# A four-layer kernel on one core: the last batch's matrix made in batch 4, batch 14's outputs in two pairs of tiles

## The chip, the core and the metric

The kernel runs on one core of one Trainium2 chip. The metric is device time in microseconds (us) of one execution, given as the median of several runs. All times below are us unless marked otherwise.

## What is computed

`x` has 16 batches of 512 rows (steps) and 512 columns (features), `cond` 16 rows of 512. Four layers follow each other, each added to its input:

```python
x = x + L0(x, cond)   # a gate from cond; the rest of the layer collapses to x * gate per batch and feature
x = x + L1(x, cond)   # recurrence: h_t = tanh(x_t @ Wx + b + h_{t-1} @ Wh), 512 steps
x = x + L2(x, cond)   # gated recurrence, written with cumulative sums over the steps
x = x + L3(x, cond)   # every batch has its own 512 x 512 matrix
```

L2 and L3, cut to what matters here (LN, GELU and biases inside `h` left out):

```python
f, i = sigmoid(x @ W_f.T + b_f), sigmoid(x @ W_i.T + b_i)
s = f + i + EPS;  f, i = f / s, i / s
new = i * (x @ W_h.T + b_h)
hidden = scans over the steps of f and new            # products and sums along time
layer[b] = base_layer + x_a[b] @ x_b[b].T             # rank 8, x_a and x_b from cond
out[b] = x[b] + x[b] @ layer[b]
```

## The kernel before

Everything is held with features on the 128 partitions, in four chunks of 128 (`KC = 4`), and steps or batches along the free dimension. `x2` (all batches, after L0 and L1) stays in SBUF as `[128, 4, 16, 512]`.

**The recurrence** takes the first 907 us. It also computes L3's factors (`x_a`, `x_b`) and parks them in DRAM, and computes the gates of L2 for the first 128 to 192 steps of each batch ("early"), which are parked in DRAM too. `made_before(b, j)` tells how many steps of batch b and feature chunk j are done so. At its end it makes the matrix of batch 0 in `wx_sb`, whose first use is over. Twice the unit matrix is added to `base_sb`'s diagonal, so that the product with it also carries the residual.

**After the recurrence** a loop over the batches works on L2 and L3. Its order is written by hand in the loop; the tile framework then places the instructions of each engine, whose order the built program fixes. The parts:

- `gate_unit(b, j, x3)`, written (b,j) here: TensorE does three groups of four matrix products into banks `pf`, `pi` and `pc0` or `pc1` (L700; `pc` alternates with j), for the steps that are not early: 384, 384, 368 and 352 columns in units 0 to 3 of batches 1 to 7, and 320 in units 0 and 1 from batch 8 on. SP loads the early steps of f and i (L715), ScalarE makes the sigmoids (L716), VectorE sums, inverts, multiplies and scans (L717 to L732; `f` has three buffers, `i` and `s` two), and GpSimd (POOL) adds (L736) and makes chunk j of `x3`, the input of L3 (L737). In the very last unit VectorE does L736 and L737.
- `layer_rows(b)`: eight small loads by SP of the factors of batch b into `at` and `bt`, which have one buffer each (L527, L528).
- `layer_of(b, at, bt, layer)`: four TensorE products (L535) of 8 rows into the banks `pl0`, `pl1`, `po0`, `po1`, and four VectorE additions of `base_sb` (L539), which write the four chunks of the batch's matrix.
- `last_layer(b, x3, layer)`: four output tiles t of 128 steps. For each, four products over the feature chunks k (L756) into bank `po0` (t even) or `po1` (t odd), a copy by ScalarE to one of two `osb` buffers (L751) and a store by SP (L752). A bank must be copied before it is written again, and an `osb` buffer stored.

PSUM has eight banks, one tile each: `pl0 pf pl1 pi po0 pc0 po1 pc1`. Where a bank is written again, its last reader must be done; where `pl` and `po` banks are used for a matrix, that reader is L539.

The order in batch b from 1 to 14: `layer_rows(b)`, (b,0), (b,1), outputs of batch b - 1, (b,2), `layer_of(b)` into `wx_sb`, (b,3). In batch 15: (15,0), `layer_rows(15)` and `layer_of(15)` into `base_sb` itself, (15,1), (15,2), (15,3), and then the outputs of batch 14. After the loop, batch 15's own outputs: three tiles and two half tiles take their first three feature chunks each (`pl_last`, `po_last`, `po_end`, `pi_end`), then each its last chunk, with copies and stores behind. ScalarE, VectorE, GpSimd and SP each run their instructions in order: a waiting one holds up all behind it.

Of the kernel before, what the change touches and what calls it, by code (L numbers as in the profile page):

```python
# [35 lines left out]
P = 128  # L36
B, S, D = 16, 512, 512
KC = D // P
# [45 lines left out]
def kernel(  # L84
# [41 lines left out]
    base_sb = keep.tile([P, KC, D], F32)  # L126
# [97 lines left out]
    with tc.tile_pool(name="ps_pre", bufs=1, space=PSUM) as ps_pre:  # L224
# [63 lines left out]
        def turned_layer(src, w_sb, which, name, between):  # L288

            ps = ps_pre.tile([P, P], F32, tag="pre", name=f"ps_{name}")  # L290
            for k in range(KC):
                for j in range(KC):
                    nc.tensor.matmul(
                        ps[j * BP : (j + 1) * BP, :],
                        src(k),
                        tile_columns(w_sb[:, k, :], j),
                        start=(k == 0),
                        stop=(k == KC - 1),
                        skip_group_check=True,
                    )  # L300
            between()
            z = pre.tile([P, KC, BP], F32, name=f"z_{name}")
            nc.vector.transpose(z, ps.rearrange("p (c f) -> p c f", c=KC))
            nc.vector.tensor_tensor(z, z, vector_of(which), ALU.add)
            gate = pre.tile([P, KC, BP], F32, name=f"gate_{name}")
            nc.scalar.activation(gate, z, AF.Sigmoid)
            return z, gate
# [26 lines left out]
        _, gate = turned_layer(lambda k: hq[:, k, :], w2_sb, C_L0B2, "g", scale)  # L334
# [189 lines left out]
    def load_layer(b, at, bt):  # L524
        for c in range(KC):
            rows = slice(c * BP, c * BP + R)
            nc.sync.dma_start(out=at[rows, :], in_=factor[0][b, :, c * P : (c + 1) * P])  # L527
            nc.sync.dma_start(out=bt[rows, :], in_=factor[1][b])  # L528
        return at, bt

    def make_layer(at, bt, banks):

        for c, pl in enumerate(banks):
            rows = slice(c * BP, c * BP + R)
            nc.tensor.matmul(pl, at[rows, :], bt[rows, :], start=True, stop=True)  # L535

    def add_base(banks, layer):
        for c, pl in enumerate(banks):
            nc.vector.tensor_tensor(layer[:, c, :], pl, base_sb[:, c, :], ALU.add)  # L539
# [25 lines left out]
    for n in range(NBLK):  # L565
        ahead = []
        if n + 2 < NBLK:
            xs.append(new_x1(n + 2))
        for s in range(T):
# [36 lines left out]
            bank, place = PLACE[g]  # L606
# [7 lines left out]
            if n == 0 and s == G - 1:  # L614
                opening.close()
                x2pool = ctx.enter_context(tc.tile_pool(name="x2pool", bufs=1, side="right"))
                x2 = x2pool.tile([P, KC, B, S], F32)
# [17 lines left out]
            if s in (1, 3) and n < 2 * KC:  # L635
# [3 lines left out]
                if i < 3 * KC:  # L639
                    m, which = divmod(i, 3)  # L640
                    w_sb, w = ((wf_sb, wfT), (wi_sb, wiT), (wc_sb, wcT))[which]
                    j = (KC - 2, KC - 1, 0, 1)[m]
                    at = slice(j * P, (j + 1) * P)
                    nc.scalar.dma_start(out=w_sb[:, :, at], in_=chunks(w)[:, :, at])
                else:
                    k = i - 3 * KC
# [44 lines left out]
    def bank(tag, name):  # L691
        return pools[tag].tile([P, D], F32, tag=tag, name=f"{tag}_{name}")
# [46 lines left out]
    def layer_rows(b):  # L739
        at = work.tile([P, P], F32, tag="at", name=f"at_{b}", bufs=1)  # L740
        bt = work.tile([P, D], F32, tag="bt", name=f"bt_{b}", bufs=1)
        return load_layer(b, at, bt)

    def layer_of(b, at, bt, layer):
        banks = [bank(tag, f"{b}_layer") for tag in ("pl0", "pl1", "po0", "po1")]
        make_layer(at, bt, banks)
        add_base(banks, layer)

    def leave(b, t, po, tag="osb"):
        osb = work.tile([P, D], F32, tag=tag, name=f"osb_{b}_{t}")  # L750
        nc.scalar.copy(osb, po)  # L751
        nc.sync.dma_start(out=out[b, t * P : (t + 1) * P, :], in_=osb)  # L752

    def output_part(po, t, x3, layer, ks):
        for k in ks:
            nc.tensor.matmul(  # L756
                po, x3[:, k, t * P : (t + 1) * P], layer[:, k, :], start=(k == 0), stop=(k == KC - 1)
            )

    def last_layer(b, x3, layer):  # L760
        for t in range(S // P):
            po = bank(f"po{t % 2}", f"{b}_{t}")
            output_part(po, t, x3, layer, range(KC))
            leave(b, t, po)

    layer = wx_sb
    pending = None
    for b in range(B):
        x3 = x3pool.tile([P, KC, S], F32, tag="x3", name=f"x3_{b}")
        end = b == B - 1  # L770
        if 0 < b < B - 1:
            factors = layer_rows(b)
        for j in range(KC):
            gate_unit(b, j, x3)
            if j == (KC - 1 if end else 1) and pending is not None:
                last_layer(*pending)
            if j == 2 and 0 < b < B - 1:
                layer_of(b, *factors, layer)
            if j == 0 and end:

                layer_of(B - 1, *layer_rows(B - 1), base_sb)
        pending = b, x3, layer


# [3 lines left out]
    columns = [slice(n * D // 2, (n + 1) * D // 2) for n in range(2)]  # L788

    def last_rows(ks, n):  # L790
        for k in ks:
            nc.tensor.matmul(
                ends[n],
                x3[:, k, last * P :],
                base_sb[:, k, columns[n]],
                start=(k == 0),
                stop=(k == KC - 1),
            )

    for t, po in enumerate(pos):  # L800
        output_part(po, t, x3, base_sb, range(KC - 1))
    for n in range(2):
        last_rows(range(KC - 1), n)

    for t, po in enumerate(pos):
        output_part(po, t, x3, base_sb, (KC - 1,))
        leave(B - 1, t, po, ("osb", "i", "s")[t])
    for n, copy in enumerate((nc.vector.tensor_copy, nc.scalar.copy)):
        last_rows((KC - 1,), n)
        osb = work.tile([P, D // 2], F32, tag=("s", "osb")[n], name=f"osb_end_{n}")  # L810
        copy(osb, ends[n])
        (nc.sync, nc.scalar)[n].dma_start(out=out[B - 1, last * P :, columns[n]], in_=osb)
# [58 lines left out]
```

## Time and profile before

| what | value |
|---|---|
| three runs, median (lowest to highest) | 1618.64 (1617.01 to 1619.62) |
| the profiled execution | 1615.84 |
| its span (first to last instruction) | 1614.1 |
| the recurrence ends, (0,0) begins on TensorE | 909.4 |
| one batch, by TensorE (batches 1 to 7, then 8 to 14) | 45.0, then 42.4 to 42.9 |
| VectorE busy, 900 to 1600, of 20 in a slice | 12.8 to 19.9 |
| granted TensorE clock | 1.00 throughout |

How to read the profile lines shown below. A group or timeline line gives the start, the duration, the engine, the source line (L539 is line 539), the operation, output <- inputs by the program's names, shapes, and the count. What stands in brackets at the end is how long the engine had been idle before it and whose end released it. PE is TensorE, DVE VectorE, ACT ScalarE, POOL GpSimd, SPq the queue of SP's transfers, whose row is the issue and not the landing. In the list of waits a line reads: engine and line that waited, `<-` engine, tile and line that ended the wait: total us, how many, the longest. Each f32 matrix product shows as two records, so x32 is sixteen products. Records of TensorE overlap a little; from start to start is the better measure.

### The profile page before, as it was taken

The numbers are of one execution on the slowest core, as the hardware profiler recorded it, in microseconds if no ns is written. First come the engines' busy times: TensorE is split into PE (matmuls) and PEld (weight loads), VectorE is DVE, ScalarE is ACT, GpSimd is POOL, SyncE is SP. The second block draws the span as 40 slices with busy tenths as digits, with TensorE's granted clock in tenths as the row PEclk, the third lists the DMA queues.
The fourth block names the chain that finished last, engine by engine and source line by source line (L and its number), as shares of the span: only waits on it lengthen the run. The fifth ranks groups of instructions, "written<-read, shape, count | busy, mean of one in ns | idle before, by whom it ended". The sixth has DMA issues, their size and how long they took to land.

```text
span 1614.1 us, 67901 instructions
## 1 busy us (share of the span) xinstructions
PE 1603.6 (99%) x29328; PEld 1146.0 (71%) x29328; DVE 1132.3 (70%) x3618; ACT 424.9 (26%) x2484; POOL 172.6 (11%) x145
## 2 busy tenths in 40 slices
PE   9999999999999999999999999999999999999998
PEld 6888888888888888888888655555555555555564
DVE  4555655565556666666665798888888888988887
ACT  3333333333333333333333211111111111111111
POOL 0000000000000000000000022222222222222222
PEclk9999999999999999999999999999999999999999
DMA  7554431111111111111111101111111111111111
GB/s 228 148 147 128 121 105 46 36 31 36 37 37 37 37 37 37 37 37 31 37 39 30 29 21 43 33 43 39 43 40 44 44 46 39 31 44 47 37 44 58
DMA packets 128085, 88.11 MB, mean 55 GB/s; under 512 B 22645, under 2 KB 116633, under 8 KB 127785
## 3 DMA queue, kind: packets, MB, share of 16 engines
q1 hardware_dynamic: 79152, 55.05, 11.1%
q10 hardware_dynamic: 48632, 28.73, 6.2%
q8 instruction: 229, 3.75, 1.0%
q14 instruction: 72, 0.58, 0.1%
HBM read 55.67 MB, written 28.07 MB: 52 GB/s over the span
## 4 chain that ended last, share of the span: by engine, by line
PE 96%; DVE 2%; DMA 1%; issue 0%; SPq 0%; ACT 0%; ACTq 0%; DVEq 0%
PE pre L417 41%; PE po L756 13%; PE pg L465 13%; PE pf L700 9%; PE pc L700 9%; PE pi L700 9%; PE pf L380 1%; PE pl_layer L535 1%; DVE s L718 1%; DMA wh_sb<-in_wh_dram 1%; PE pl_last L756 0%; DMA xb<-in_xT_dram 0%; DVE s L726 0%; DVE s L730 0%; PE po_last L756 0%
## 5 line engine op out<-in xcount | busy, mean ns | idle before, releaser
L417 PEld LDWEIGHTS pre<-wh_sb,h_out 128*32 128x32 f32 x16384 | 466.7, 110 | 146.6 <-DVE h_out L610 143.4
L417 PE MATMUL pre<-wh_sb,h_out 128*32 128x128 f32 x16384 | 560.6, 273 | 2.4 <-DVE h_out L610 1.1
L610 DVE STREAM_TRANSPOSE h_out<-a 128x32 f32<-128x32 f32 x2048 | 264.6, 187 | 347.4 <-ACT a L609 345.9
L609 ACT ACTIVATE a<-pre 128x32 f32<-128x32 f32 x2048 | 238.0, 203 | 573.4 <-PE pre L417 572.7
L417 PE MATMUL pre<-wx_sb,x 128*32 128x128 f32 x8192 | 285.9, 273 | 1.0 <-DMA wx_sb<-in_wx_dram 0.5
L417 PEld LDWEIGHTS pre<-wx_sb,x 128*32 128x32 f32 x8192 | 239.0, 110 | 2.1 <-DMA wx_sb<-in_wx_dram 1.5
L756 PE MATMUL po<-wx_sb,x 128*128 128x512 f32 x480 | 209.0, 592 | 0.1
L756 PEld LDWEIGHTS po<-wx_sb,x 128*128 128x128 f32 x480 | 91.0, 190 | 111.6 <-issue 105.7
L700 PE MATMUL pf<-x,wf_sb 128*128 128x352 f32 (+3 forms) x512 | 165.3, 466 | 0.3 <-DVE x L622 0.3
L700 PE MATMUL pc<-x,wc_sb 128*128 128x352 f32 (+3 forms) x512 | 163.7, 463 | 1.3 <-DVE i L722 1.3
L700 PE MATMUL pi<-x,wi_sb 128*128 128x352 f32 (+3 forms) x512 | 163.6, 462 | 0.0
L718 DVE RECIPROCAL s<-s 128x368 f32<-128x368 f32 (+2 forms) x64 | 152.2, 2378 | 2.2
L700 PEld LDWEIGHTS pf<-x,wf_sb 128*128 128x128 f32 x512 | 96.0, 190 | 68.4 <-issue 15.8
L736 POOL TENSOR_TENSOR s<-s,f 128x512 f32<-128x512 f32 x63 | 86.5, 1374 | 509.9 <-DVE s L730 504.1
L700 PEld LDWEIGHTS pc<-x,wc_sb 128*128 128x128 f32 x512 | 97.2, 190 | 57.5 <-DVE i L722 1.9
L700 PEld LDWEIGHTS pi<-x,wi_sb 128*128 128x128 f32 x512 | 97.3, 190 | 55.9
L622 DVE TENSOR_TENSOR x<-x,h_out 128x128 f32<-128x128 f32 x256 | 101.2, 395 | 18.9 <-DMA wi_sb<-in_wiT_dram 0.2
L751 ACT COPY osb<-po 128x512 f32<-128x512 f32 x60 | 35.1, 585 | 263.4 <-PE po L756 144.9
L683 POOL MEMSET zero<- 128x1 f32 x1 | 0.1, 98 | 907.5 <-DVE wx_sb L539 907.5
L717 DVE SCALAR_TENSOR_TENSOR s<-f,i 128x368 f32<-128x368 f32 (+2 forms) x64 | 34.7, 543 | 88.1 <-ACT i L716 88.1
L716 ACT ACTIVATE f<-pf,vec_sb 128x368 f32<-128x368 f32 (+2 forms) x64 | 35.7, 558 | 215.2 <-PE pf L700 160.6
L465 PE MATMUL pg<-x,wc_sb 128*32 128x512 f32 (+1 forms) x640 | 84.2, 581 | 0.0
(113 smaller groups left out, 1270.8 us busy)
## 6 DMA issues: line engine op xcount, KB each, us to landing
out_dram<-osb SPq DMA_DIRECT2D x63, 256.0 KB
xb<-in_xT_dram ACTq DMA_DIRECT2D x61, 256.0 KB
w<-in_l3w_dram SPq DMA_DIRECT2D x72, 128.0 KB
w<-in_l3w_dram ACTq DMA_DIRECT2D x64, 128.0 KB
early<-ef SPq DMA_DIRECT2D x39, 128.0 KB
early<-ei SPq DMA_DIRECT2D x39, 128.0 KB
f<-early SPq DMA_DIRECT2D x16, 96.0 KB
i<-early SPq DMA_DIRECT2D x16, 96.0 KB
```

The lines of the kernel that those rows point to most:

```text
L417: nc.tensor.matmul(pre[PLACE[g][0]][j * BP : (j + 1) * BP, PLACE[g][1], :], lhsT, tile_columns(w, j), start=False, stop=False, skip_group_ ...
L465: nc.tensor.matmul(ps[c * BP : (c + 1) * BP, :].rearrange("p (b t) -> p b t", **shape), w[:, k, j * P + c * BP : j * P + (c + 1) * BP], x2 ...
L609: nc.scalar.activation(a[:, at], pre[bank][:, place, at], AF.Tanh)
L610: nc.vector.transpose(turned[:, c, :], a[:, at])
L622: nc.vector.tensor_tensor(x2[:, :, :, at].rearrange("p k b t -> p k t b"), xs[n][:, :, t0 // 2, :, :], turned.rearrange("p k (t b) -> p k ...
L700: nc.tensor.matmul(p[:, te:], w_sb[:, k, j * P : (j + 1) * P], x2[:, k, b, te:], start=(k == 0), stop=(k == KC - 1),)
L716: nc.scalar.activation(gate[:, new], p[:, new], AF.Sigmoid, bias=col(bias, j))
L717: nc.vector.scalar_tensor_tensor(s[:, new], f[:, new], EPS, i[:, new], ALU.add, ALU.add)
L718: nc.vector.reciprocal(s[:, new], s[:, new])
L736: engine.tensor_tensor(s, s, f, ALU.add)
L751: nc.scalar.copy(osb, po)
L756: nc.tensor.matmul(po, x3[:, k, t * P : (t + 1) * P], layer[:, k, :], start=(k == 0), stop=(k == KC - 1))
```

## The change

Three parts:

1. The matrix of batch 15 is made in batch 4, behind (4,0), and is written to `last_matrix`, which is the part of `x2` that held batch 0 (no longer needed after batch 0). Its eight loads stand at the head of batch 4, and batch 4's own eight loads come behind it; in the other batches `layer_rows(b)` is written behind (b,0) and no longer ahead of it. Batch 15's outputs read `last_matrix`; `base_sb` keeps its value.
2. The outputs of batch 14 come in two pairs of tiles: tiles 0 and 1 behind (15,1), tiles 2 and 3 behind (15,2), and none behind (15,3).
3. `last_layer` takes a pair of tiles. In the first pair the product with the last feature chunk of tile 0 comes behind the first two products of tile 1, so that `x3`'s last chunk is read two products later.

```diff
@@ -757,28 +757,40 @@
                 po, x3[:, k, t * P : (t + 1) * P], layer[:, k, :], start=(k == 0), stop=(k == KC - 1)
             )
 
-    def last_layer(b, x3, layer):
-        for t in range(S // P):
-            po = bank(f"po{t % 2}", f"{b}_{t}")
-            output_part(po, t, x3, layer, range(KC))
-            leave(b, t, po)
+    def last_layer(b, x3, layer, rows):
+
+        t = rows[0]
+        po = [bank(f"po{n}", f"{b}_{t + n}") for n in range(2)]
+        ahead = 0 if t else 2
+        output_part(po[0], t, x3, layer, range(KC - 1))
+        output_part(po[1], t + 1, x3, layer, range(ahead))
+        output_part(po[0], t, x3, layer, (KC - 1,))
+        leave(b, t, po[0])
+        output_part(po[1], t + 1, x3, layer, range(ahead, KC))
+        leave(b, t + 1, po[1])
 
     layer = wx_sb
+    last_matrix = x2[:, :, 0, :]
+
+
+    when = ({1: ((0, 1), (2, 3))}, {1: ((0, 1),), 2: ((2, 3),)})
     pending = None
     for b in range(B):
         x3 = x3pool.tile([P, KC, S], F32, tag="x3", name=f"x3_{b}")
         end = b == B - 1
-        if 0 < b < B - 1:
-            factors = layer_rows(b)
+
+        extra = layer_rows(B - 1) if b == KC else None
         for j in range(KC):
             gate_unit(b, j, x3)
-            if j == (KC - 1 if end else 1) and pending is not None:
-                last_layer(*pending)
+            if extra and j == 0:
+                layer_of(B - 1, *extra, last_matrix)
+            if j == 0 and 0 < b < B - 1:
+                factors = layer_rows(b)
+            if pending is not None:
+                for rows in when[end].get(j, ()):
+                    last_layer(*pending, rows)
             if j == 2 and 0 < b < B - 1:
                 layer_of(b, *factors, layer)
-            if j == 0 and end:
-
-                layer_of(B - 1, *layer_rows(B - 1), base_sb)
         pending = b, x3, layer
 
 
@@ -792,18 +804,18 @@
             nc.tensor.matmul(
                 ends[n],
                 x3[:, k, last * P :],
-                base_sb[:, k, columns[n]],
+                last_matrix[:, k, columns[n]],
                 start=(k == 0),
                 stop=(k == KC - 1),
             )
 
     for t, po in enumerate(pos):
-        output_part(po, t, x3, base_sb, range(KC - 1))
+        output_part(po, t, x3, last_matrix, range(KC - 1))
     for n in range(2):
         last_rows(range(KC - 1), n)
 
     for t, po in enumerate(pos):
-        output_part(po, t, x3, base_sb, (KC - 1,))
+        output_part(po, t, x3, last_matrix, (KC - 1,))
         leave(B - 1, t, po, ("osb", "i", "s")[t])
     for n, copy in enumerate((nc.vector.tensor_copy, nc.scalar.copy)):
         last_rows((KC - 1,), n)
```

## Prediction

> (b,j) is gate unit j of batch b, tile t one of a batch's four output tiles.
>
> **What bounds the kernel now.** I read the page first, then TensorE's waits after the recurrence (from 915 us), then both engines' timelines at the two places that the change touches.
>
> ```profile
> PE 1603.6 (99%) x29328; PEld 1146.0 (71%) x29328; DVE 1132.3 (70%) x3618; ACT 424.9 (26%) x2484; POOL 172.6 (11%) x145
> ...
> PE 96%; DVE 2%; DMA 1%; issue 0%; SPq 0%; ACT 0%; ACTq 0%; DVEq 0%
> ```
>
> ```profile
> PE pc L700 <- DVE i L722: 1.3, 1, 1.3
> ```
>
> TensorE is busy throughout and 96% of the chain that ended last. After the recurrence one wait is listed, 1.3 us. So an edit pays only by removing one of TensorE's few gaps, and any new gap is paid in full. The one gap, in TensorE's timeline of batch 15:
>
> ```profile
> 1556.90 2.32 PE L700 MATMUL pc<-x,wc_sb 128*128 128x320 f32 x8
> 1559.15 0.70 PE L535 MATMUL pl_layer<-bt,at 8*128 8x512 f32 x2
> ...
> 1560.22 2.42 PE L700 MATMUL pf<-x,wf_sb 128*128 128x320 f32 x8
> 1562.48 2.32 PE L700 MATMUL pi<-x,wi_sb 128*128 128x320 f32 x8
> ...
> 1576.57 2.53 PE L700 MATMUL pi<-x,wi_sb 128*128 128x352 f32 x8
> 1580.39 2.63 PE L700 MATMUL pc<-x,wc_sb 128*128 128x352 f32 x8 [1.29 <-DVE i L722]
> 1582.86 13.90 PE L756 MATMUL po<-wx_sb,x 128*128 128x512 f32 x32
> 1596.60 5.31 PE L756 MATMUL pl_last<-base_sb,x 128*128 128x512 f32 x12
> ...
> 1606.91 1.88 PE L756 MATMUL pl_last<-base_sb,x 128*128 128x512 f32 x4
> ```
>
> First column start, second length. Four gate units run with no output work between them; VectorE falls behind, and pc of (15,3) waits until L722 of (15,1) has read its bank.
>
> Now batch 4, which the change makes like it: TensorE, then VectorE.
>
> ```profile
> 1079.64 2.74 PE L700 MATMUL pc<-x,wc_sb 128*128 128x384 f32 x8
> 1082.22 2.74 PE L700 MATMUL pf<-x,wf_sb 128*128 128x384 f32 x8
> ...
> 1089.96 13.90 PE L756 MATMUL po<-wx_sb,x 128*128 128x512 f32 x32
> 1103.69 2.64 PE L700 MATMUL pf<-x,wf_sb 128*128 128x368 f32 x8
> ```
>
> ```profile
> 1073.26 1.20 DVE L730 TENSOR_TENSOR_SCAN s<-i,zero 128x512 f32<-128x512 f32 x1
> 1074.37 1.26 DVE L539 TENSOR_TENSOR wx_sb<-po_layer,base_sb 128x512 f32<-128x512 f32 x2
> 1075.55 0.64 DVE L717 SCALAR_TENSOR_TENSOR s<-f,i 128x352 f32<-128x352 f32 x1
> ...
> 1084.49 0.54 DVE L717 SCALAR_TENSOR_TENSOR s<-f,i 128x384 f32<-128x384 f32 x1
> ...
> 1092.51 1.20 DVE L730 TENSOR_TENSOR_SCAN s<-i,zero 128x512 f32<-128x512 f32 x1
> ```
>
> VectorE has no idle time here. It starts (4,0) only at 1084.49, when TensorE has had those products done for 2.3 us, and ends its last scan 1.2 us after 1092.51, while TensorE already writes po0 from 1089.96.
>
> **Part 1, the last matrix in batch 4.** *TensorE's four L535 products* move. In batch 15 they cost 1.28: pc to pf is 3.32 where a 320-wide group takes 2.15 (+1.17), pf to pi 2.26 (+0.11). So +1.28 in batch 4, -1.28 in batch 15. Eight loads move with them; the batch 4 loads that stand there today leave at 1067.5 to 1070.2, and L535 comes at 1082.2. Batch 4's own eight loads go behind an f load that waits for POOL, at about 1086, needed at about 1116: free.
>
> *The new wait.* The matrix products take banks po0 and po1; they are free again when the last two L539 have run, and the order of the built program puts those behind the whole VectorE chain of (4,0), after L730. In the old place nothing asked for po0 until three units later. Now the outputs of batch 3 ask after one unit: at 1089.96 + 1.28 = 1091.24. VectorE: in unit (3,2) an L539 behind the reciprocal cost 0.43 (2.92 from L718 to L719, against 2.49 in (15,2) without), one behind L726 0.46 (1.71 against 1.25). L730 of (4,0) moves from 1092.51 to 1093.40; the pair begins 1.11 later, 1094.51; the first takes 0.66 (0.63 to 0.67 alone): 1095.17, and TensorE goes on 0.05 later, as it does behind L722 in batch 15. **Wait 3.98**, plus 0.10 for slow first products (pc of (15,3) took 2.47, not 2.37): **+4.08**. Behind the waiting product stand all outputs of batch 3 and units (4,2), (4,3); nothing hides it. VectorE's own 2.07 (0.43 + 0.46 + 1.18) vanishes: it idles 6.6 us before (4,2). Bounds: 0 if the pair ran in time; above, the twin in batch 15, where the first po bank came free 16.1 us after L535 (1559.15 to 1575.29), while batch 4 asks 1.28 + 7.74 = 9.0 after it: 7.1 + 0.1. I take 4.08, since batch 4's own rows give it.
>
> No row has a TensorE gap that long: the longest are 1.3 us, and the granted clock is 1.00 in every slice. [...]
>
> *Reading the matrix from x2* instead of base_sb changes no shape: 0.
>
> **Part 2, batch 14's outputs in two pairs.** TensorE's new order from (15,0) at 1552.60: 6.45 + 6.45 (320-wide units), 6.87 (half of 13.73), 7.41, 6.87, 7.11, then the last batch's first three features, 10.31 (1596.60 to 1606.91): 1604.07. Before, 1606.91: **-2.84**, of which 1.28 is the moved matrix and 1.55 the L722 wait with its slow restart. What comes late next? pc of (15,3) is asked at 1591.4; L722 of (15,1) is done near 1578. VectorE, without its four L539: (15,1) begins 1573.9 and (15,2) 1582.5 (8.57 each); (15,3) waits for its i sigmoid, about 1592.2. From there to x3 took 10.33 (1593.39 to 1603.72), so 1602.6: 1.5 ahead of 1604.07. If that cover went, each us beyond it would cost one. The pair's second copy needs its buffer's store, issued behind the i load at 1582.9 and landed 2.3 later; the product ends at 1586.7.
>
> **Part 3, last features later.** Only batches 13 and 14 wait for x3: outputs take 14.03 and 14.04 there, 13.73 elsewhere. The new order asks 1.72 later, so both 0.30 go. But they are not the bound there. L717 of unit 2 comes at 1459.51, 1502.38, 1545.33: 42.9 apart, where TensorE's own batch is 42.44. That ring runs VectorE, POOL, SP's f load, the store of tile 1, ScalarE's copy of tile 3, its sigmoids, VectorE:
>
> ```profile
> 1541.32 3.33 SPq L752 DMA_DIRECT2D out_dram<-osb  x3
> ```
>
> ```profile
> 1543.70 0.58 ACT L751 COPY osb<-po 128x512 f32<-128x512 f32 x1 [7.88 <-DMA out_dram<-osb]
> ```
>
> The layer product into po1 waits for that copy (0.13 in batch 13, 0.20 in 14). TensorE will come 0.30 earlier and wait longer: **0**; bounds 0 to -0.93 (both waits, both pairs).
>
> In batches 1 to 7 SP now holds the store of tile 0 behind the i load of unit 3 (1050.75 to about 1058.2 in batch 3). It lands near 1060.5; the copy of tile 3 waits for the store of tile 1, 1061.91, as before, and the i sigmoid behind has 0.87 spare: 0.
>
> **Sum:** 1.28 + 4.08 - 2.84 = **+2.5 us**. The profiled execution took 1615.84 (span 1614.1) and would take 1618.4; the three runs' median is 2.8 higher, 1618.64, so I forecast **1621.2**.
>
> **Rivals.** *VectorE is later in batch 4* (slower). One mechanism: the stores of tiles 0 and 1 now leave 1.4 us apart instead of 9; if they delay each other by over 0.87, ScalarE's sigmoids and VectorE's start of (3,2) move, and each us adds one to the po wait. From 0.7 us the total is over +0.2%. For: landings vary (the copy in batch 12 came 2.93 after its issue, against 2.3 elsewhere). Against: the 0.87. Price, if VectorE is as late as in batch 15: wait 7.2, +5.7, 1624.3. Chance 0.24.
>
> *No wait at po0* (the pair of L539 runs in time): 1.28 - 2.84 = -1.6, 1617.1. For: TensorE's wait list knows no such wait today. Against: the built order and VectorE's unbroken rows. 0.12.
>
> *The end gives nothing back but the matrix* (x3 over 1.5 late): 4.08 + 1.28 - 1.28 = +4.1, 1622.7. 0.06.
>
> Forecast: 0.58, its own range 1619.6 to 1622.8.
>
> **Numbers.** 0.2% is 3.2 us, about what a measurement of this kernel can tell from no change. Slower: a fifth of the forecast's chance (its centre is 0.7 short of the line and the runs spread 2.6), nearly all of the first rival, most of the third: 0.38. Faster: a few parts of the second, 0.03. Same: 0.59. Range 1617.0 to 1624.6, from no wait to the twin.
>
> **What would show it.** Right: TensorE's wait list has po L756 <- DVE L539 once, near 4 us, at about 1091; pc <- L722 is gone; outputs of batches 13 and 14 take 13.7 and their layer products wait longer; the last k = 3 products begin about 2.5 later than 1606.91. Wrong: no po wait, or one of 5 and more; a clock below 1.00 behind it; a wait for x3 before the last products.

## The result, and the profile after

| | before | after |
|---|---|---|
| five runs of each, median (lowest to highest) | 1617.99 (1617.01 to 1619.62) | 1625.44 (1623.54 to 1627.23) |
| the profiled execution | 1615.84 | 1623.54 |
| its span | 1614.1 | 1621.8 |
| (0,0) begins on TensorE | 909.40 | 912.78 |
| first of the last k = 3 products | 1606.91 | 1614.46 |

The ratio is 1.0045 (95% interval 1.0034 to 1.0057): slower by 7.45 us, where +2.5 was forecast, and outside the range. Of the 7.7 between the profiled executions, 3.38 are there before the changed code begins: the recurrence, which is the same in both, ended that much later. What the change itself does is better read from the stretch between the table's last two rows, called **the stretch** below: 697.51 before, 701.68 after, **+4.17** against +2.52 forecast.

The page of the changed kernel, busy times and the share of the chain that ended last, and TensorE's waits behind the recurrence:

```profile
PE 1607.0 (99%) x29327; PEld 1147.4 (71%) x29328; DVE 1132.9 (70%) x3618; ACT 425.3 (26%) x2484; POOL 172.8 (11%) x145
...
PE 97%; DMA 1%; DVE 1%; issue 0%; ACT 0%; SPq 0%; POOL 0%; ACTq 0%
```

```profile
PE po L756 <- DVE x L539: 3.9, 1, 3.9
```

The wait for L722 is gone and one for L539 stands in its place: the one forecast, three times as long as the one removed. TensorE and then VectorE in batch 4 (3.38 later than the lines of before, by the recurrence):

```profile
1083.02 2.74 PE L700 MATMUL pc<-x,wc_sb 128*128 128x384 f32 x8
...
1086.77 2.85 PE L700 MATMUL pf<-x,wf_sb 128*128 128x384 f32 x8
...
1092.03 2.74 PE L700 MATMUL pc<-x,wc_sb 128*128 128x384 f32 x8
1098.67 15.67 PE L756 MATMUL po<-wx_sb,x 128*128 128x512 f32 x32 [3.90 <-DVE x L539]
1114.18 2.64 PE L700 MATMUL pf<-x,wf_sb 128*128 128x368 f32 x8
```

```profile
1096.75 1.20 DVE L730 TENSOR_TENSOR_SCAN s<-i,zero 128x512 f32<-128x512 f32 x1
1097.87 1.26 DVE L539 TENSOR_TENSOR x<-po_layer,base_sb 128x512 f32<-128x512 f32 x2
```

From the start of pc, 2.58 for its products gives 1094.61; the outputs start at 1098.67, after the first of the pair at 1097.87 has read po0: a wait of 4.06. But look at the length of those outputs: 15.51 from start to start (1098.67 to 1114.18), where the same sixteen products took 13.73 before. The wait ended and TensorE was still slower. TensorE in 1-us windows there (length, busy share, granted clock, then DMA share and GB/s):

```profile
1099.00:1100.00 1.00, 1.00 (x3) 1.00 0.26 68
1100.00:1101.00 1.00, 1.00 (x3) 0.53 0.35 82
...
1103.00:1104.00 1.00, 1.00 (x3) 0.76 0.00 0
1104.00:1105.00 1.00, 1.00 (x4) 1.00 0.00 0
```

The clock falls to half (0.50), and only 1.4 us after products have begun again. The two windows left out show 0.50. The lost parts, 0.47 + 0.50 + 0.50 + 0.24 = 1.71, are all but 0.07 of the 1.78 by which the outputs are longer. The page hides this: its slice of 40 us still shows 9 tenths, and the mean clock is 0.999.

The end of batch 15:

```profile
1562.97 2.32 PE L700 MATMUL pf<-x,wf_sb 128*128 128x320 f32 x8
...
1614.46 1.88 PE L756 MATMUL pl_last<-x,x 128*128 128x512 f32 x4
```

No wait is listed here any more: 51.49 from (15,0) to the last k = 3 products, 54.31 before, -2.82.

So the stretch adds up from rows of both traces: +1.27 (the moved matrix: 3.75 from pc to pf where 2.58 is a group, and 2.68 for the next) + 4.06 (wait) + 1.78 (half clock) - 2.82 (end) = +4.29, against 4.17.

### The profile page after: what moved, and what is told of

It is laid out like the page before. It is cut to its first block, busy times and chain, and to the rows that moved or that the text cites. A ratio compares the mean times of both kernels' runs of the same rounds, so it can differ in the third digit from the quotient of the medians.

```text
span 1621.8 us, 67894 instructions
## 1 busy us (share of the span) xinstructions
PE 1607.0 (99%) x29327; PEld 1147.4 (71%) x29328; DVE 1132.9 (70%) x3618; ACT 425.3 (26%) x2484; POOL 172.8 (11%) x145
## 3 DMA queue, kind: packets, MB, share of 16 engines
q8 instruction: 229, 3.75, 1.0%
## 4 chain that ended last, share of the span: by engine, by line
PE 97%; DMA 1%; DVE 1%; issue 0%; ACT 0%; SPq 0%; POOL 0%; ACTq 0%
PE pre L417 41%; PE po L756 13%; PE pg L465 13%; PE pf L700 9%; PE pi L700 9%; PE pc L700 9%; PE pf L380 1%; PE pl_layer L535 1%; DMA xb<-in_xT_dram 1%; PE pl_last L756 0%; DMA wx_sb<-in_wx_dram 0%; PE po_last L756 0%; DVE s L726 0%; DVE s L730 0%; PE po_layer L535 0%
## 5 line engine op out<-in xcount | busy, mean ns | idle before, releaser
L417 PE MATMUL pre<-wh_sb,h_out 128*32 128x128 f32 x16384 | 568.3, 273 | 2.4 <-DVE h_out L610 1.1
L417 PE MATMUL pre<-wx_sb,x 128*32 128x128 f32 x8192 | 291.2, 273 | 2.3 <-issue 1.1
L417 PEld LDWEIGHTS pre<-wx_sb,x 128*32 128x32 f32 x8192 | 244.1, 110 | 3.8 <-issue 1.3
L465 PE MATMUL pg<-x,wi_sb 128*32 128x512 f32 (+1 forms) x640 | 85.7, 582 | 0.0
```

What stands on the lines that cost most here:

```text
L417: nc.tensor.matmul(pre[PLACE[g][0]][j * BP : (j + 1) * BP, PLACE[g][1], :], lhsT, tile_columns(w, j), start=False, stop=False, skip_group_ ...
L465: nc.tensor.matmul(ps[c * BP : (c + 1) * BP, :].rearrange("p (b t) -> p b t", **shape), w[:, k, j * P + c * BP : j * P + (c + 1) * BP], x2 ...
```

## The experiments

**Theory.** The wait at po0 costs what was forecast; the step that failed is the clock, for which the forecast has no term: behind the gap of 3.9 it was at 0.50, and that adds 1.7 to 2.5 us. The 3.4 us of the recurrence are scatter between executions. **Rivals.** The recurrence is slower because of the change; the longer outputs come from something else in batch 4 (transfers, reading the matrix from x2); the half clock comes by chance and not by the gap.

All results in one table. "Gap" is the listed wait at po0, "outputs" the length of batch 3's sixteen products behind it, in e_p2 of the first pair of batch 14. A single execution is marked so.

| run | gap | outputs | (0,0) at | stretch | time | ratio to before |
|---|---|---|---|---|---|---|
| before | none | 13.73 | 909.40 | 697.51 | 1617.99 | |
| before_again | none | 13.73 | 912.64 | 697.35 | 1618.91 (one) | |
| after | 3.90 | 15.51 | 912.78 | 701.68 | 1625.44 | 1.0045 (1.0034 to 1.0057) |
| after_again | 3.92 | 16.26 | 912.26 | 702.51 | 1623.14 | 1.0031 (1.0020 to 1.0042) |
| e_fill | 0.46 | 13.81 | 910.72 | 699.50 | 1619.74 | 1.0016 (1.0006 to 1.0025) |
| e_fill1 | 3.05 | 15.27 | 911.54 | 701.18 | 1623.35 (one) | |
| e_fill2 | 2.20 | 13.81 | 909.26 | 699.96 | 1618.17 (one) | |
| e_swap | none | 13.73 | 909.86 | 695.93 | 1616.13 | 0.9990 (0.9982 to 0.9999) |
| e_p1swap | none | 13.73 | 909.93 | 696.51 | 1615.37 (one) | |
| e_p2 | 8.49 | 8.77, not 6.87 | 911.01 | 706.05 | 1625.99 (one) | |
| e_p3 | none | 13.73 | 909.05 | 697.10 | 1615.42 (one) | |
| e_swap_osb3 | none | 13.73 | 912.83 | 694.93 | 1614.23 | 0.9976 (0.9967 to 0.9985) |

### Both kernels again

Nothing edited; this asks whether the late end of the recurrence belongs to the change.

> The kernel before once more, unchanged. In the first profile its first gate product after the recurrence began at 909.4; the changed kernel's at 912.8, although no instruction of the recurrence was changed. Theory A (scatter between executions): the start of that product varies by 2 to 4 us from run to run of the same program. Theory B (the change shifts the recurrence): it is again within 0.5 us of 909.4, and the span near 1614. Both: after that product the part to the end is 704.7 again, within 0.5.

> The changed kernel once more. Both theories: the part behind the recurrence is longer than before by 4.3 (1.28 for the moved matrix + 4.06 wait at po0 + 1.78 half clock behind it - 2.83 at the end), or by 2.5 where the half clock does not come. Theory A (the start of the first gate product is scatter): it begins anywhere from 909 to 913. Theory B (the change shifts the recurrence): again near 912.8. By A the timed median is 4 to 6 over before, by B 7 to 8.

The kernel before, run again, begins (0,0) at 912.64, as late as the changed one does, while its stretch agrees with the first to 0.16. So the 3.38 are scatter: over all rows of the table that start lies between 909.05 and 912.83, with either code. The two kernels differ by 1.0031 here, about 5 us, and the profiled stretches by 5.16.

In the second profile of the changed kernel the half clock lasts longer:

```profile
1098.16 16.42 PE L756 MATMUL po<-wx_sb,x 128*128 128x512 f32 x32 [3.92 <-DVE x L539]
```

```profile
1096.00:1097.00 1.00, 0.00 (x0) 0.64 0.03 8
...
1103.00:1104.00 1.00, 1.00 (x3) 0.95 0.00 0
```

The same gap, 3.92 and 3.90, but here the clock falls inside it; products meet about 4.9 us of half clock and not 3.4, and the outputs take 2.53 more and not 1.78.

### The gap filled with products of no use (e_fill, e_fill1, e_fill2)

The wait stays, but TensorE works in it. The products go to a bank that is free, and nothing reads them.

```diff
...
+            if extra and j == 1:
+                spare = bank("pl0", "spare")
+                for _ in range(FILL):
+                    nc.tensor.matmul(spare, wf_sb[:, 0, :P], wf_sb[:, 0, :], start=True, stop=True)
             if pending is not None:
                 for rows in when[end].get(j, ()):
```

Four of them (FILL = 4):

> The changed kernel, and four products of no use (512 columns, about 3.4 us, bank pl0) ahead of batch 3's outputs, so that TensorE works where it waited. Theory C (the slow outputs behind the wait come from TensorE's idle gap): the outputs of batch 3 take 13.7 again and not 15.5, the granted clock stays at 1.00, and the part behind the recurrence is shorter than the changed kernel's by about 1.7, in spite of more work. Rival (VectorE's writes or the new operand slow those outputs): they take 15.5 again.

One:

> The changed kernel with one product of no use in the wait instead of four: TensorE's gap is about 3.2 instead of 4.06 (two profiles of the changed kernel) and 0.5 (four products). [...] Theory 2 (a shorter gap is enough): half clock for 3 to 7 us and outputs of 15.5 to 17.

Two:

> Two products of no use ahead of batch 3's outputs. Their work stands inside the wait, so the stretch without a product should be about 2.2 to 2.35 us (3.0 with one, 0.5 with four). Theory (a gap of about 3 us brings the half clock, one of 1.3 does not): between them this one decides where. If 2.3 us is enough, batch 3's outputs take 15 to 16.5 us and the start of the recurrence to the first of the last k=3 products is about 701; if it isn't, they take 13.7 to 13.9 at a clock of 1.00 and that stretch is about 699.5, as with four. Rival (the half clock comes by chance and not by the gap): a half clock also where no gap stands, or none here and at 3 us in one run of several.

The sixteen outputs of batch 3 in each, in this order, with the wait that is left in brackets:

```profile
1096.60 13.97 PE L756 MATMUL po<-wx_sb,x 128*128 128x512 f32 x32 [0.46 <-DVE x L539]
```

```profile
1097.43 15.43 PE L756 MATMUL po<-wx_sb,x 128*128 128x512 f32 x32 [3.05 <-DVE x L539]
```

```profile
1095.17 13.97 PE L756 MATMUL po<-wx_sb,x 128*128 128x512 f32 x32 [2.20 <-DVE x L539]
```

Counted from (0,0), they start as late as in the changed kernel (185.9). To the next start they take 13.81 with a gap of 0.46 (mean clock of the execution 1.000) or 2.20 (1.00 in every 1-us window from 1085 to 1108), and 15.27 with 3.05, where the clock is 0.50 from 1096.97 to 1100.38. The 0.08 over 13.73 that is left with the clock held is the slow first products of the forecast.

This takes the second rival away: the moved loads, the matrix in x2 and the wait itself are all still there, and the outputs take their 13.8. It also tests the forecast's own sum with the clock held: the mean of the two stretches of before, 697.43, + 2.52 is 699.95; two products give 699.96, four 699.50. Timed, four products are 1.0016 of before. By the medians, taken on the same chip, useless products make the changed kernel faster: 1619.74 against 1623.14. One thing in e_fill1 is left unexplained: its tail behind the first of the last k = 3 products was some 1.7 longer than in the other two, although TensorE and ScalarE's copies took no longer there; what is longer lies behind the last copy.

### The banks exchanged (e_swap)

What makes TensorE wait is that po0 and po1 take the matrix's last two columns. Here they take its first two, whose L539 run early, and pl0 and pl1, which nobody asks for soon, the last two.

```diff
-    def layer_of(b, at, bt, layer):
-        banks = [bank(tag, f"{b}_layer") for tag in ("pl0", "pl1", "po0", "po1")]
+    def layer_of(b, at, bt, layer, tags=("pl0", "pl1", "po0", "po1")):
+        banks = [bank(tag, f"{b}_layer") for tag in tags]
...
-                layer_of(B - 1, *extra, last_matrix)
+                layer_of(B - 1, *extra, last_matrix, ("po0", "po1", "pl0", "pl1"))
```

> The changed kernel, but the matrix of batch 15 takes its banks in the order po0, po1, pl0, pl1, so that VectorE frees po0 behind its reciprocal and po1 behind its first scan, and no longer last. My theory: the wait of outputs on L539 (4.06) and the half clock behind it (1.78) are gone, the end keeps its 2.83: the part behind the recurrence is 1.5 to 1.6 shorter than before's 704.7, so 703.1. Rival (the loss is the matrix's place, its loads or the order of the stores, not the bank): it stays at 707 or more.

The outputs of batch 3 now follow pc of (4,1) without a gap, at full clock (1.000, the mean of the profiled execution):

```profile
1089.11 2.74 PE L700 MATMUL pc<-x,wc_sb 128*128 128x384 f32 x8
1091.69 13.90 PE L756 MATMUL po<-wx_sb,x 128*128 128x512 f32 x32
```

TensorE's list has no wait left in L2 and L3, the stretch is 695.93, 1.50 under the mean of before: the rival "no wait at po0" of the prediction, -1.6, made on purpose. Against the changed kernel that is 5.75 to 6.58 for an exchange of four names; 4.06 of it is the wait and 1.78 to 2.53 the clock, 5.84 to 6.59 together.

### The matrix without the pairs (e_p1swap)

As e_swap, but batch 14's outputs stay in one group behind (15,3). It splits e_swap's gain; part 3 is in both.

```diff
-    when = ({1: ((0, 1), (2, 3))}, {1: ((0, 1),), 2: ((2, 3),)})
+    when = ({1: ((0, 1), (2, 3))}, {3: ((0, 1), (2, 3))})
```

> The matrix in batch 4 with the two pairs of banks exchanged there, batch 14's outputs left in one group behind the last unit of batch 15 as before, last features late. Theory: no wait at po0 in batch 4, no half clock, the matrix of batch 15 no longer behind its first unit, the wait of the first matrix of batch 15's end for a bank shorter (about 0.6 instead of 1.45): start of the recurrence to the first of the last k=3 products about 696.7, to the end of the span about 703.8, so half of the gain of the exchange is the matrix's and half the pairs'. Rival (the gain of the exchange is all from the pairs of outputs): the two stretches are those of before, 697.4 and 704.6.

```profile
1579.92 2.63 PE L700 MATMUL pc<-x,wc_sb 128*128 128x352 f32 x8 [0.58 <-DVE i L722]
```

Its pi begins at 1576.81. From pi to pc it takes 3.11, where a group of 352 takes 2.36: 0.75 of waiting, 1.46 before (3.82). Counted from (15,0), VectorE, without four L539 at that place, frees the bank 1.97 earlier than before, and TensorE asks for it 1.26 earlier. The stretch of 696.51 is 0.92 under before's mean, e_swap's 1.50. But 0.27 of the 0.58 between them lies ahead of (15,0), where the two kernels are the same: scatter. From (15,0) to the last k = 3 products it is 54.31 before, 52.34 here and 51.49 in e_swap: the moved matrix takes 1.97 off the end and costs 1.27 in batch 4, a gain of 0.70, and the two pairs bring 0.85. That is about half each, from single profiles.

### The pairs alone (e_p2)

The kernel before with the outputs of batch 14 in two pairs; the matrix of batch 15 stays behind (15,0).

```diff
-    def last_layer(b, x3, layer):
-        for t in range(S // P):
+    def last_layer(b, x3, layer, rows):
+        for t in rows:
...
+    when = ({1: (range(S // P),)}, {1: ((0, 1),), 2: ((2, 3),)})
...
```

> The kernel before with part 2 alone: batch 14's outputs in two pairs behind (15,1) and (15,2), while the matrix of batch 15 is still made behind (15,0) with po0 and po1 third and fourth. My theory: the outputs ask for po0 about 8.6 before VectorE frees it (L535 at 1559.2, free 16.1 later, asked 7.5 later), the clock is halved behind that gap, and the part from the first gate product to the end is 7 + 1.7 to 3.4 longer, 713.3 to 715. Without the half clock 711.6. Rival (the pairs pay by themselves): 703 to 704.

```profile
1576.59 8.93 PE L756 MATMUL po<-wx_sb,x 128*128 128x512 f32 x16 [8.49 <-DVE base_sb L539]
1585.36 2.64 PE L700 MATMUL pf<-x,wf_sb 128*128 128x368 f32 x8
```

The same wait at the place that the prediction called the twin, 8.49 long, and behind it 8.77 for eight products that take 6.87: the half clock again, +1.90. To the end of the span it is 713.19 from (0,0), at the lower edge of what the half clock was expected to give and 1.6 above what the wait alone would. Part 2 thus needs part 1: without the move, and with the banks in this order, the pairs cost 8.6.

### Part 3 alone (e_p3), and the ring broken (e_swap_osb3)

e_p3 is the kernel before with the last feature of tile 0 behind two products of tile 1, and nothing else.

> The kernel before with part 3 alone: tiles in pairs, and the last feature chunk of tile 0 behind the first two products of tile 1; nothing else. My theory (the ring over VectorE, the store and ScalarE's copy bounds batches 13 and 14): the outputs of batches 13 and 14 take 13.7 instead of 14.03, the layer products into po1 there wait 0.43 instead of 0.13 and 0.20, and the part from the first gate product to the end stays at 704.6, within 0.2. Rival (the wait for x3 was lost time): it is 0.6 shorter, 704.0.

The outputs of batches 13 and 14 take 13.73, and no longer 14.03: the x3 wait is gone. The layer products into po1 then wait 0.21 and 0.42. The stretch is 697.10, 0.25 to 0.41 less than in the two profiles of before, which themselves lie 0.16 apart. The rows agree with that: the outputs save 0.61 in the two batches, and the longer waits take 0.30 of it back. So part of the x3 wait was lost time here and part was given back; it leans to the ring and doesn't settle it.

e_swap_osb3 is e_swap with three buffers for the copies. The small tile `at` moves into one that has served its time, to make room.

```diff
-        at = work.tile([P, P], F32, tag="at", name=f"at_{b}", bufs=1)
+        at = ident
...
-        osb = work.tile([P, D], F32, tag=tag, name=f"osb_{b}_{t}")
+        osb = work.tile([P, D], F32, tag=tag, name=f"osb_{b}_{t}", bufs=3 if tag == "osb" else 2)
...
```

> The version with the swapped banks, and three buffers instead of two for the output copies (the small factor tile takes the place of the unit matrix, to make room). Theory (the ring runs over the store of tile 1, for which tile 3's copy waits): the copies wait for no store, the layer products of batches 13 and 14 wait no longer (0.43 each in the changed kernel), and the part from the first gate product to the end is 0.8 to 0.9 shorter than with swapped banks alone: 702.1 instead of 703.0. Rival (VectorE's own work is the ring): 703.0.

ScalarE's third and fourth copy of one batch's outputs, in the changed kernel and then here (the first two begin at 1538.42 and 1540.13, here at 1532.14 and 1533.86):

```profile
1545.61 0.59 ACT L751 COPY osb<-po 128x512 f32<-128x512 f32 x1 [4.89 <-DMA out_dram<-osb]
1554.08 0.59 ACT L751 COPY osb<-po 128x512 f32<-128x512 f32 x1 [7.88 <-DMA out_dram<-osb]
```

```profile
1537.30 0.59 ACT L751 COPY osb<-po 128x512 f32<-128x512 f32 x1 [2.85 <-PE po L756]
1540.73 0.59 ACT L751 COPY osb<-po 128x512 f32<-128x512 f32 x1 [2.85 <-PE po L756]
```

With two buffers the third and fourth copy wait 4.89 and 7.88 for stores to land, and the sigmoids behind the fourth begin at 1554.56 and 1555.02, straight after it, although TensorE had begun their products at 1546.76 and the next group at 1551.70. With three, every copy waits for TensorE alone and the fourth is done 8.6 after the first and not 15.7. The layer products of batches 13 and 14 take 0.52, the batches 42.44, and the stretch falls by a further 1.00. The ring was real, and this is the fastest version of the study: 0.9976 (0.9967 to 0.9985) of the kernel before.

### What a gap does to the clock (e_gaps)

The third rival, chance, was still open: the gap of 2.20 was one sample, and the two of 3.9 had cost 1.78 and 2.53. This kernel is the one before with a series of measurements behind its end, so its time is not compared; only the clock around 47 gaps of known length is read.

```diff
...
+    for g in range(GAPS):
+        n = 128 + 8 * g
+        for m in range(28 + g % 5):
+            pb = bank(f"pc{m % 2}", f"burst_{g}_{m}")
+            nc.tensor.matmul(pb, wf_sb[:, m % KC, :P], half, start=True, stop=True)
+        nc.vector.tensor_scalar(two[:, :n], pb[:, :n], 0.0, 2.0, ALU.mult, ALU.add)
+        nc.vector.reciprocal(half[:, :n], two[:, :n])
```

> The kernel before, with a series of measurements behind its end: 48 bursts of 28 to 32 products of no use (12 to 14 us each), and between them gaps on TensorE that VectorE makes by reading the last product and inverting 128 to 504 columns, so that the gaps grow from about 1.3 to about 4.3 us. The time is longer by all this and is not compared; only the granted clock around each gap is read. What the runs so far show: half clocks of 3.42, 3.41 and 6.83 us, all multiples of 3.41, and in the changed kernel run again the one in the start-up and the one in batch 4 begin 316.0 times 3.413 apart. Theory (windows of 3.41 us that run by themselves, and a window with less than some 40% of products halves the next): all half clocks of this run begin on one grid of 3.413 us; gaps under 1.9 us bring none, gaps over 4.1 all do, and between them it goes by how the gap lies on the grid: at 2.3 us about a quarter, at 3.0 about two thirds; the window ahead of each half clock has over 2.0 us without a product. Rival (the length of the gap alone decides, with a limit between 2.2 and 3.05 us): gaps over the limit all bring it, those under it never, and the beginnings lie on no grid.

The bursts took 24 to 30 us, not 12 to 14 (a product of this size is 0.86 long), and the gaps went from 1.52 to 4.14.

| gaps | 1.5 to 1.95 | 1.95 to 2.5 | 2.5 to 3.1 | 3.1 to 3.6 | 3.6 to 4.2 |
|---|---|---|---|---|---|
| how many | 9 | 9 | 11 | 8 | 10 |
| with half clock | 0 | 4 | 10 | 5 | 10 |

Length alone does not decide: 1.99 and 2.22 brought it and 2.57, 3.15, 3.27 and 3.56 did not. The place on a grid does: all 29 half clocks of this run begin on one grid of 3.413 us, to 0.01, and last 3.41 or 6.83. Cut by that grid, the shares of the gaps in single windows at full clock part at 2.0: every window with 2.03 us or more without a product is followed by a half clock, no window with 1.94 or less is, and of the two between, 1.99 was and 2.01 was not. And a half clock ended after its first window where TensorE stood for up to 0.26 us in it, and only after the second where it stood for 0.73 and more. Three windows on the grid, around the shortest gap that brought it (1.99 us, all in the first):

```profile
1884.46:1887.87 3.41, 1.42 (x5) 1.00 0.00 0
1887.87:1891.29 3.42, 3.42 (x6) 0.50 0.00 0
1891.29:1894.70 3.41, 3.41 (x10) 1.00 0.00 0
```

So the theory holds in this run, with a limit of 2.0 us of 3.41 for these products. The rival of a limit on the length falls; what is chance here is only where the gap lies on the grid. The forecast's shares (a quarter at 2.3 us, two thirds at 3.0) were too low and about right.

The runs before this one agree. In the changed kernel the half clock begins at 1100.06, so its windows meet at 1096.65: the gap, 1094.77 to 1098.67, is cut into 1.88, which does nothing, and 2.02, which does. In the second profile the cut is at 1096.28: 2.04 and 1.88; the first brings the half clock, the second keeps it for another window (6.83 us in all). In e_p2 it is 1.93, which does nothing, and then a whole window. In e_fill2 nothing comes of the 2.20; where the grid cuts them is not shown, as no half clock marks it there.

An estimate, worked out from e_gaps' two limits (2.0 us, and between 0.26 and 0.73) over all places of the grid: a gap of 3.9 brings the half clock in 97 of 100 cases and costs 1.4 to 3.1 us where it does, about 2 on average; one of 2.2 brings it in 47 of 100 and costs 0.8 on average over all; one under 2.0 none. The 2.20 of e_fill2 could as well have gone the other way.

## Why the prediction was wrong

**The step that failed** is the last one on part 1: the gap's effect on the clock. The sum has no term for it: no row of before had such a gap (the longest are 1.3), and with the clock at 1.00 in every slice none showed a price. A clock below 1.00 behind the wait stood among its own signs of being wrong, and it came: in the profiles of the changed kernel the outputs took 1.78 and 2.53 more, behind e_p2's gap of 8.49 1.90 more, and the estimate from e_gaps' limits for this gap is about 2. Of the 1.78 and 2.53, the 0.10 for slow first products stands in the sum already. With the rest it is 2.52 + 1.68 to 2.43 = 4.20 to 4.95; the measured stretches are +4.25 and +5.08 over before's mean. The range had no part for the clock either: its upper end was the twin's wait alone.

**What lay outside the sum.** Forecast plus clock is 1622.9 to 1623.6. The median of the second comparison, 1623.14, agrees; that of the first, 1625.44, is some 2 us longer. Its profiled execution was the lowest of its five and had the late recurrence already. The mean granted clock is on record for all five: 0.999 in the profiled one, with its single window of 3.41 us at half clock, and 0.996 to 0.998 in the other four (0.997 to 0.999 in the second comparison). One such window takes 0.001 off the mean, so by estimate the four had about two to four. Where these lay, in batch 4 or in the start-up, left no trace and stays open, and so does whether they are the whole of the 2 us.

**The wait at po0**: right in place, cause and size, 4.06 against 3.98; the slow first products, 0.08 with the clock held (e_fill, e_fill2), against 0.10. The order of VectorE's instructions around it held to 0.05: L730 was worked out for 1093.40, which with 3.38 is 1096.78, and came at 1096.75.

**The moved matrix**: 1.27 against 1.28. **The end of batch 15**: -2.82 against -2.84; x3 came in time, and no wait for it stands before the last products.

**Part 3 at nothing**: right in the changed kernel. The outputs of 13 and 14 are 0.30 shorter each (13.73), and their layer products wait 0.44 and 0.43, where it had been 0.13 and 0.20, so some 0.07 is left. Alone (e_p3) only half came back. That the ring runs over the store and ScalarE's copy is shown by e_swap_osb3.

**Rivals.** VectorE was not later in batch 4 than forecast; the wait was 3.9 and not 7.2. The third did not come. The second, no wait, needed the exchange of banks.

## What to carry to other kernels

In this kernel a gap on TensorE had two prices, its length and what the clock did behind it. In e_gaps none of the nine gaps up to 1.93 us brought a half clock, and all ten from 3.6 us on did; behind the 3.9 of the changed kernel the outputs took 1.78 and 2.53 us more in two profiles, so that even products of no use in the gap paid (e_fill, 1619.74 against 1623.14). When work is moved to an earlier place, look at which bank each part uses and who asks for that bank next; giving the banks that are wanted soon to the parts that are read first took the whole cost away here. Compare two profiles from a mark behind the unchanged part, not from zero: here 3.4 of 7.7 us lay ahead of it.

## What the runs showed of the hardware

What e_gaps shows of the clock was not in the prediction: half clocks on a grid of 3.413 us, each after a window with 2.0 us or more without products, and full clock again after a window with little (0.26, and 0.46 in e_fill1, were little enough; 0.73 was not). So the half clock could begin when products had resumed, 1.4 us after in the changed kernel, and the same gap cost 1.78 in one execution and 2.53 in the next. In the changed kernel run again, one half clock lies in the start-up, from 17.67, and one in batch 4, from 1096.28: 316.0 windows of 3.4133 apart.

The start of the kernel shows a half clock too, with the code unchanged, while the first loads arrive. TensorE in windows of 2 us, in the second profile of before:

```profile
16.00:18.00 2.00, 1.15 (x20) 0.67 1.13 322
18.00:20.00 2.00, 2.00 (x45) 0.50 0.78 249
```

In the first profile of before these windows show 1.00. The longest gap ahead of it is 1.42 us, of which 1.27 lie in the window of the grid before the half clock, with others of 0.26, 0.35 and 0.14: several short ones add up, here to 2.0. In the changed kernel run again the window ahead of 17.67 holds gaps of 0.27, 0.21 and 1.72: 2.2. The weights there have 32 columns (128*32 in the rows) and not 128; whether the limit of e_gaps holds for them to the tenth is not shown. In e_swap_osb3 the mean clock of the profiled execution is 0.998 although TensorE's list has no wait in L2 and L3: at the 0.001 of one window, an estimated two of half clock elsewhere. Over 24 executions of the kernel before on one chip, the six with a mean clock of 1.000 took 1615.74 to 1617.82 and the seven with 0.998 or less 1618.04 to 1620.68. So part of the scatter of this kernel goes with the clock; whether all of it does stays open.
